# Tiles of their own for the first two inverse Haar sums, their places in the order, and earlier loads of the next coefficients

## Chip, cores and metric

One core of a Trainium2 chip. The metric is the device time of one execution in microseconds; the median of three runs is given. Engines are named as in the profile: PE (TensorE matmul), PEld (its weight loads), DVE (VectorE), ACT (ScalarE), POOL (GpSimd), SP (the queue that issues all DMAs here).

## What is computed

Four layers on a float32 image stack of 4 x 64 channels x 256 x 256. Layers 0, 2 and 3 are long 2D convolutions, separable per channel, with a residual; layer 1 is a Haar transform, a per-coefficient channel mixing with soft threshold, and the inverse transform:

```python
# layers 0, 2, 3: filters hx, hy come from small sine networks
k   = hx outer hy                          # one 256 x 256 filter per channel
y   = irfft2(rfft2(x) * rfft2(k))[:256, :256]
out = y + x * bias

# layer 1
f1 = haar2d(x)
for i in range(2):
    f4  = einsum('bchw,oc->bohw', f1 * v[i], conv_w[i])
    acc = acc + sign(f4) * relu(abs(f4) - tau[i])
out = haar2d(acc, inverse=True) + x
```

## The kernel before

**Rounds and groups.** Images are worked on in 64 rounds of 2 channels by 2 images (a tile `[128, 8, 256]`, 1 MB). Rounds 0 to 31 are group 0 (two images), 32 to 63 group 1. The channel mixing needs all channels of a group, so the coefficients go through DRAM: `coef[group]` before it, `mixed[group]` after it.

**Three phases**, each a list of small pieces that emit instructions:

- `phase_a`, the forward part, ten pieces a round (`A_PIECES`). In round t: convolution along rows of round t (`rows`, PE `a1ps`, evicted by ACT to `ay`), the Haar product of round t-3 (`product`, PE `a3ps`, evicted on DVE at L477 to `f`), convolution along columns of round t-1 (`columns`, PE `a2ps`, residual on DVE at L464 to `x1`), and, on POOL, the sums and differences of the Haar transform along the free dimension of round t-2 (`forward_free`, L344 and L346, 16 instructions, tiles `h128` to `h2`, result `fw`). The tail pieces are `a_last` (round 64, with the products of rounds 61 and 62, no rows any more) and `a_end` (forward sums and product of round 63, stores of 62 and 63).
- `phase_b(group)`, the mixing: load `ft` from `coef` and `v`/`tau`, matmul with the mixing matrix (L607), multiply, sign, magnitude, subtract, threshold (DVE and ACT), add on POOL, store to `mixed` (L675). It starts with a `join` of two steps on DVE (L579 to L586). Its pools are `b` and `bps` for group 0, `b2` and `bps2` for group 1.
- `phase_c`, the inverse part, 18 pieces a round (`C_PIECES`): load `g` from `mixed` (L755), scale it on ACT from round 2 on (`scales`, L362), the sums of the inverse Haar transform along the free dimension (`inverse_free`, 16 instructions in 8 levels, result `ci`), Haar product (PE `c0ps`, evicted by ACT to `z`), rows and columns of layer 2 (`c1r`, evicted to `ch`; `c1c`, residual to `cy`), the same for layer 3 (`c2r`, `c2c`), store. For rounds 0 and 1 the inverse sums run on DVE (L387, scaling inside), for later ones on POOL (L385).

**Order.** Each engine executes its instructions in the order in which they were emitted, and waits at the head of its queue. `beside(main, side, lead, tail)` emits a list of pieces and spreads a second list evenly among them. Most evictions are put off to the next piece (`later`, `flush`). The chain of calls at the end of the kernel is: forward pieces beside the filter networks; forward pieces beside the mixing of group 0; the last two rounds of forward pieces (62 and 63), with the first inverse rounds' loads and sums (`c_before`) among them; `a_last`; then the mixing of group 1 beside the inverse rounds.

**Buffers.** A tag of a pool is a ring of `bufs` tiles; a new tile waits until the last user of the one that it replaces has finished. What matters here:

- `in` (3): `x_t` of the forward rounds, then `g_t`, 1 MB each.
- `h2` to `h128` (1 each): the levels of `forward_free` *and* of `inverse_free`.
- PSUM: `acps`, a ring of 4 banks; `wide` or `wide2`, 2 banks more while they are open, taken in every third request; `bps`/`bps2` for the mixing.
- `v` (3), `m` (3), `x` (2) of pool `b`: the mixing's own, idle once it has ended.

`c_before` is `start` (load g_0 and g_1, the first Toeplitz filters, set up the sums of rounds 0 and 1) followed by eight lots of four inverse sums. `start` is emitted after piece (63, 3), the lots after pieces (63, 4) to (63, 7) and beside `a_last`. g_2 and g_3 are loaded in pieces 0 and 4 of inverse round 0.

Of the kernel before, what the change touches and what calls it, by code (L numbers as in the profile page):

```python
# [41 lines left out]
F32 = mybir.dt.float32  # L42
# [5 lines left out]
P = 128  # L48
B, C, N = 4, 64, 256

ROW = 64
BLOCKS = N // ROW
HALF = N // 2
# [13 lines left out]
NB = B // GROUPS  # L67
CI = 4 // NB
M = CI * NB
# [8 lines left out]
A_PIECES = 2 * BLOCKS + 2  # L78
C_PIECES = 4 * BLOCKS + 2
AHEAD = 3  # L80
SHRINK = (1, 2, 3, 5, 6, 10, 11, 12, 14, 15)
W = 2 * N
# [16 lines left out]
def conv_haar_kernel(  # L99
    ctx: ExitStack, tc: tile.TileContext, x, zT, w1, wbd, cols, wo, decay, wo_first, decay_first, bias, forward, inverse, wrow, pack, v, v_rows, out  # L100
):
    nc = tc.nc
# [15 lines left out]
    def pool(name, bufs, stack=ctx, **kw):  # L118
        return stack.enter_context(tc.tile_pool(name=name, bufs=bufs, reuse_waits="tile", **kw))

    ac = pool("ac", 2)
    acps = pool("acps", 4, space=PSUM)

    def big(tag, name, bufs):
        return ac.tile([P, 2 * M, N], F32, tag=tag, name=name, bufs=bufs)
# [24 lines left out]
    def load_toeplitz(l, t):  # L150

        both = ac.tile([P, SPAN - ROW], F32, tag="toep", name=f"toep{l}_{t}", bufs=4)
        for r in range(2):
            start = filt[l].offset + (t % ROUNDS * 2 + r) * REPEATS * SPAN
            src = bass.AP(filt[l].tensor, start, [[SPAN - 4, 16], [SPAN - 1, 4], [1, SPAN - ROW]])
            nc.sync.dma_start(both[r * ROW : (r + 1) * ROW], src)
        return both
# [122 lines left out]
    rest = []  # L282
# [68 lines left out]
    def diffs(src, half):  # L351

        if half < BLOCKS:
            return src.rearrange("p n (k q) -> p n k q", k=BLOCKS)[:, :, half : 2 * half, 0]
        m = half // BLOCKS
        return src.rearrange("p n (k q) -> p (n k) q", k=BLOCKS)[:, :, m : 2 * m]

    def scales(src):

        half = 2  # L360
        while half < N:
            nc.scalar.mul(diffs(src, half), diffs(src, half), math.sqrt(half))  # L362
            yield
            half *= 2

    def inverse_free(src, dst, name, engine):


        blocks = src.rearrange("p n (k q) -> p n k q", k=BLOCKS)

        cur, half = blocks[:, :, 0:1, 0], 1
        while half < N:
            o = dst
            if half < HALF:
                o = ac.tile([P, 2 * M, 2 * half], F32, tag=f"h{2 * half}", name=f"{name}{2 * half}", bufs=1)
            d = diffs(src, half)
            if half < BLOCKS:
                s, pair = cur, o.rearrange("p n (t q) -> p n t q", q=2)
            else:
                s = cur.rearrange("p n (k t) -> p (n k) t", k=BLOCKS)  # L380
                pair = o.rearrange("p n (k t q) -> p (n k) t q", k=BLOCKS, q=2)
            for q, op in ((0, ALU.add), (1, ALU.subtract)):
                to = pair[:, :, :, q]
                if engine is nc.gpsimd:
                    engine.tensor_tensor(to, s, d, op)  # L385
                else:
                    engine.scalar_tensor_tensor(to, d, math.sqrt(half) * (1 - 2 * q), s, ALU.mult, ALU.add)  # L387
                yield
            cur = o
            half *= 2  # L390
# [13 lines left out]
    def run(ops, count):  # L404
        for _ in range(count):
            next(ops, None)

    def all_rows(grp_tile, r, images, joined):

        parts = images.rearrange("(m q) (h n) k -> q m h (n k)", q=2, h=2)  # L410
        n = NB * W
        pairs = []
        for q in range(2):
            for h in (slice(0, 2),) if joined else (slice(0, 1), slice(1, 2)):
                at = grp_tile.offset + ((h.start * 2 + q) * ROUNDS + r) * n
                rows = [[PAIR, P // 2], [2 * ROUNDS * n, h.stop - h.start], [1, n]]
                pairs.append((bass.AP(grp_tile.tensor, at, rows), parts[q][:, h]))
        return pairs
# [321 lines left out]
    def phase_c():  # L740
# [3 lines left out]
        alone = total - ROUNDS  # L744
        stores = []
        st = [dict() for _ in range(total)]

        def load(t, k=slice(0, 4)):
            if t >= total:
                return  # L750
            if k.start == 0:
                st[t]["g"] = big("in", f"g_{t}", 3)
                st[t]["scales"] = scales(st[t]["g"])
            for rows, g in all_rows(mixed[t // ROUNDS], t % ROUNDS, st[t]["g"], False)[k]:
                nc.sync.dma_start(g, rows)  # L755
# [49 lines left out]
        def filters(t, l):  # L805
            if t < total:
                st[t]["toep", l] = load_toeplitz(l, t)

        def sums(t):
            if t < total:  # L810
                s = st[t]
                if t >= alone:
                    for h in range(2):
                        to, of = (s[k].rearrange("p (s n) k -> p s (n k)", s=2)[:, h] for k in ("g", "shrunk"))
                        nc.gpsimd.tensor_tensor(to, to, of, ALU.add)
                s["ci"] = big("t1", f"ci_{t}", 2)
                s["ops"] = inverse_free(s["g"], s["ci"], f"i{t}_", nc.vector if t < 2 else nc.gpsimd)

        def step(t, count):
            if t < total:  # L820
                run(st[t]["ops"], count)
# [62 lines left out]
        def piece(t, j):  # L884
            flush()
            if j == 0:
                if t == 0:
                    load(2)
                sums(t + 2)
            if t == 0 or t >= alone - AHEAD:  # L890
                if j == (BLOCKS if t == 0 else 1):
                    load(t + 3)
            elif j in (1, 3, 5, 7):
                load(t + 3, slice(j // 2, j // 2 + 1))
            if stores and j == C2 + BLOCKS + 3:
                stores.pop(0)()
            if j == 2:
                filters(t + 1, 1)
            if j == C2 + BLOCKS + 1 and t > 1:
                store(t - 2)  # L900
            if j == R2 + BLOCKS:
                filters(t, 2)
            first = t == alone - AHEAD
            if t >= alone - AHEAD:
                if j == 0 and first:
                    load_raw(alone)
                    load_rows()
                if j == 2 and first:
                    scale_rows()
                if j == BLOCKS + 1:  # L910
                    load_raw(t + AHEAD + 1)
                shrink(t + AHEAD, j - 2 * first)
            if R1 <= j < R1 + BLOCKS:
                if t < total:
                    rows(t, 1, j - R1)
            elif C2 <= j < C2 + BLOCKS:
                if 1 < t:
                    columns(t - 2, 2, j - C2)
            elif R2 <= j < R2 + BLOCKS:
                if 0 < t <= total:  # L920
                    rows(t - 1, 2, j - R2)
            elif j >= C1:
                if t < total:
                    columns(t, 1, j - C1)
            else:
                product(t + 1, int(j > BLOCKS))
            if t == 0:
                scaled(3, 2 * (2 * BLOCKS <= j < C1))
                scaled(2, int(j > 0))
            else:  # L930
                scaled(t + 3, {11: 3, 12: 2, 15: 1, 16: 1}.get(j, 0))
            if j > 0:
                step(t + 2, 1)
# [5 lines left out]
            sums(0)  # L939
            sums(1)  # L940

        before = [start] + [lambda t=t: step(t, 4) for t in range(2) for _ in range(4)]
        haar_first = [lambda h=h: (flush(), product(0, h)) for h in range(2)]

        pieces = [lambda t=t, j=j: piece(t, j) for t in range(total + 2) for j in range(C_PIECES)]
# [3 lines left out]
    def beside(main, side, lead, tail, weights=(1,)):  # L949


        weights = [weights[k % len(weights)] for k in range(len(main))]
        all_of = sum(weights[lead : len(main) - tail])
        done = 0
        for k, p in enumerate(main):
            p()
            want = len(side) * sum(weights[lead : k + 1]) // max(1, all_of)
            for q in side[done:want]:
                q()
            done = max(done, want)  # L960
# [4 lines left out]
    cut_a, cut_c = (ROUNDS + 2) * A_PIECES + BLOCKS + 4, (ROUNDS - AHEAD) * C_PIECES  # L965
# [4 lines left out]
    bp = pool("b", 2, during)  # L970
# [1 line left out]

    beside(a[cut_a : -2 * A_PIECES], phase_b(0), 2, 0)

    a, head = a[-2 * A_PIECES :], A_PIECES + BLOCKS
    beside(a[:head], c_before[:1], A_PIECES - 1, 0)
    beside(a[head:], c_before[1:5], 0, 2)
    beside(a_last, c_before[5:], 0, 5)
    during.close()
    bp = pool("b2", 2, during)  # L980
    rings[:] = [acps, acps, pool("wide2", 2, space=PSUM)]
    bps = pool("bps2", 2, during, space=PSUM)

    mid = 3 * BLOCKS + 2
    main = c_first + a_end[:1] + c[:BLOCKS] + c[mid:C_PIECES] + a_end[1:] + c[BLOCKS:mid] + c[C_PIECES:cut_c]
    beside(main, phase_b(1), len(c_first) + len(a_end) + 2 * BLOCKS, 0)
    during.close()
    late["sb"] = pool("late", 1)
    late["ps"] = pool("late_ps", 1, space=PSUM)
# [124 lines left out]
```

## Time and profile before

| | |
|---|---|
| runs, median (lowest to highest) | 2587.52 us (2584.11 to 2591.82) |
| profiled execution | 2585.35 us, span 2583.6 us |
| PE busy | 2319.3 us, 90% |
| POOL busy | 2064.4 us, 80% |
| DVE busy | 1823.0 us, 71% |
| ACT busy | 1324.7 us, 51% |
| DMA | 685.23 MB, 265 GB/s mean |
| chain that ended last | PE 60%, DVE 14%, POOL 10%, DMA 6%, issue 5% |

The busy shares are averages over the whole span. The mixing of group 0 ends at about 1065 us and the first mixing matmul of group 1 starts at 1161.42 us; the change concerns the stretch between. A timeline row gives start, length, engine, line, operation, output and input, count, and in brackets the idle time before it and what ended that.

### The profile page before, as it was taken

The numbers are of one execution on the slowest core, as the hardware profiler recorded it, in microseconds if no ns is written. First come the engines' busy times: TensorE is split into PE (matmuls) and PEld (weight loads), VectorE is DVE, ScalarE is ACT, GpSimd is POOL, SyncE is SP. The second block draws the span as 40 slices with busy tenths as digits, with TensorE's granted clock in tenths as the row PEclk, the third lists the DMA queues.
The fourth block names the chain that finished last, engine by engine and source line by source line (L and its number), as shares of the span: only waits on it lengthen the run. The fifth ranks groups of instructions, "written<-read, shape, count | busy, mean of one in ns | idle before, by whom it ended". The sixth has DMA issues, their size and how long they took to land.

```text
span 2583.6 us, 118458 instructions
## 1 busy us (share of the span) xinstructions
PE 2319.3 (90%) x53292; PEld 1848.1 (72%) x53292; DVE 1823.0 (71%) x2049; ACT 1324.7 (51%) x2187; POOL 2064.4 (80%) x2428
## 2 busy tenths in 40 slices
PE   5999999678888888757999999999989999999999
PEld 4877877444444444546777778777789998999998
DVE  2555445799999999646677777766757777777763
ACT  1221212566666666325666666666655655655552
POOL 1898887899989999767676777766779999999991
PEclk8999999899999999978999999999999999999999
DMA  7676998699999999555988999988876666666653
GB/s 210 216 244 234 298 309 283 243 342 323 337 340 316 351 321 330 182 194 194 331 301 309 317 320 323 313 306 297 288 233 211 223 213 212 221 216 208 219 166 111
DMA packets 203676, 685.23 MB, mean 265 GB/s; under 512 B 29289, under 2 KB 30826, under 8 KB 190755
## 3 DMA queue, kind: packets, MB, share of 16 engines
q1 hardware_dynamic: 203171, 677.67, 77.1%
q8 instruction: 418, 6.85, 1.1%
q14 instruction: 87, 0.71, 0.1%
HBM read 427.93 MB, written 249.63 MB: 262 GB/s over the span
## 4 chain that ended last, share of the span: by engine, by line
PE 60%; DVE 14%; POOL 10%; DMA 6%; issue 5%; ACT 3%; SPq 2%; DVEq 0%; ACTq 0%; POOLq 0%
PE c2c L296 11%; PE c2r L296 10%; PE c1r L296 9%; PE c1c L296 9%; PE a1ps L296 6%; PE a2ps L296 6%; PE f L607 4%; PE c0ps L308 4%; POOL fw L344 3%; DVE m L651 3%; POOL f L346 3%; DVE x L626 3%; DVE a L646 2%; PE a3ps L308 2%; DVE x L464 2%
## 5 line engine op out<-in xcount | busy, mean ns | idle before, releaser
L385 POOL TENSOR_TENSOR i<-i,g 128x16 f32<-128x16 f32 x744 | 431.5, 601 | 27.7 <-ACT g L362 0.6
L296 PEld LDWEIGHTS a2ps<-toep,ay 64*64 64x64 f32 x8192 | 305.5, 137 | 163.9 <-DVE f L477 86.4
L296 PE MATMUL a2ps<-toep,ay 64*64 64x128 f32 (+3 forms) x8192 | 357.7, 306 | 47.9 <-DVE f L477 42.3
L607 PE MATMUL f<-ft,mix 64*64 64x512 f32 x2048 | 297.3, 617 | 111.6 <-DVE x L626 94.3
L296 PEld LDWEIGHTS a1ps<-toep,x 64*64 64x64 f32 x8192 | 288.4, 134 | 89.7 <-issue 45.4
L296 PE MATMUL a1ps<-toep,x 64*64 64x64 f32 (+3 forms) x8192 | 337.6, 300 | 16.6 <-DMA x<-in_x 11.4
L296 PEld LDWEIGHTS c2c<-toep,ch 64*64 64x64 f32 x8192 | 300.0, 135 | 58.9 <-issue 19.1
L296 PE MATMUL c1r<-toep,z 64*64 64x192 f32 (+3 forms) x8192 | 319.0, 300 | 22.6 <-issue 11.9
L296 PEld LDWEIGHTS c1c<-toep,ch 64*64 64x64 f32 x8192 | 296.2, 134 | 57.8 <-issue 18.5
L296 PEld LDWEIGHTS c1r<-toep,z 64*64 64x64 f32 x8192 | 292.4, 135 | 59.2 <-issue 28.0
L296 PE MATMUL c2c<-toep,ch 64*64 64x256 f32 (+3 forms) x8192 | 314.7, 299 | 8.4 <-ACT ch L848 6.8
L296 PE MATMUL c1c<-toep,ch 64*64 64x128 f32 (+3 forms) x8192 | 310.3, 298 | 9.0 <-ACT ch L848 5.5
L669 POOL TENSOR_TENSOR gt<-m,ft 128x512 f32<-128x512 f32 x128 | 163.5, 1277 | 193.7 <-DVE m L651 188.8
L385 POOL TENSOR_TENSOR ci<-i,g 128x1024 f32<-128x1024 f32 x124 | 313.9, 2552 | 4.5
L444 ACT COPY ay<-a1ps 128x512 f32<-128x512 f32 x256 | 137.4, 589 | 351.2 <-PE a1ps L296 350.6
L296 PEld LDWEIGHTS c2r<-toep,cy 64*64 64x64 f32 x8192 | 287.9, 134 | 32.9 <-issue 15.2
L632 ACT ACTIVATE m<-x 128x1024 f32<-128x1024 f32 x194 | 206.1, 1062 | 205.3 <-DVE x L626 98.5
L296 PE MATMUL c2r<-toep,cy 64*64 64x192 f32 (+3 forms) x8192 | 310.1, 297 | 1.3 <-issue 1.1
L848 ACT COPY ch<-c2r 128x512 f32<-128x512 f32 x256 | 137.3, 591 | 280.2 <-PE c2r L296 279.5
L477 DVE TENSOR_TENSOR f<-a3ps,wrow_sb 128x512 f32<-128x512 f32 x256 | 161.3, 683 | 130.2 <-PE a3ps L308 130.2
L626 DVE TENSOR_TENSOR x<-f,v 128x1024 f32<-128x1024 f32 x192 | 233.5, 1216 | 22.1 <-PE f L607 20.5
L344 POOL TENSOR_TENSOR fw<-x 128x1024 f32<-128x1024 f32 x64 | 122.2, 1910 | 150.4 <-DVE x L464 137.9
(83 smaller groups left out, 3976.8 us busy)
## 6 DMA issues: line engine op xcount, KB each, us to landing
toep<-filt SPq DMA_DIRECT2D x384, 224.0 KB, 5.3
ft<-coef SPq DMA_DIRECT2D x128, 512.0 KB, 7.6
v<-in_v SPq DMA_DIRECT2D x64, 1024.0 KB, 10.1
mixed<-gt SPq DMA_DIRECT2D x128, 512.0 KB, 7.2
g<-mixed SPq DMA_DIRECT2D x256, 256.0 KB, 5.1
x<-in_x SPq DMA_DIRECT2D x128, 256.0 KB, 4.4
coef<-f SPq DMA_DIRECT2D x128, 256.0 KB, 4.0
x<-in_x SPq DMA_DIRECT2D x32, 1024.0 KB, 8.0
```

The costliest lines, as they stand in the source:

```text
L296: nc.tensor.matmul(ps[r][half(c), j % 2, k * ROW :], data[half(r), c, k, bass.ts(j, ROW)], t(r, c)[:, : N - k * ROW], start=k == 0, stop=k ...
L308: nc.tensor.matmul(ps[r][half(c)].rearrange("p h k -> p (h k)"), matrix[half(r)], pairs(r, c).rearrange("p h k -> p (h k)"), start=True, s ...
L344: nc.gpsimd.tensor_tensor(diffs, even, odd, ALU.subtract)
L346: nc.gpsimd.tensor_tensor(sums, even, odd, ALU.add)
L385: engine.tensor_tensor(to, s, d, op)
L444: later(lambda y=y, ps=ps: nc.scalar.copy(y, ps))
L477: later(lambda f=f, ps=ps, w=w: nc.vector.tensor_tensor(f, ps, w, ALU.mult))
L607: nc.tensor.matmul(un[u]["f4"][half(q), b, :], mixers[0][half(r), bass.ts(i, C)], st[s]["f"][half(r), b], start=True, stop=True, tile_posi ...
L626: nc.vector.tensor_tensor(un[u]["x"], un[u]["f4"], both(u, "v"), ALU.mult)
L632: nc.scalar.activation(un[u]["m"], un[u]["x"], AF.Sign)
L669: nc.gpsimd.tensor_tensor(g[:, 0], m[:, 0], st[s]["f"][:, 0], ALU.add)
L848: later(lambda y=y, ps=ps: nc.scalar.copy(y, ps))
```

## The change

- `inverse_free` takes a function `level(n)` that gives the tile of each level. For rounds 0 and 1 the levels are cut out of tiles with the tags `m` (level 128) and `x` (levels 2 to 64) of pool `b`; for later rounds they are the `h` tiles as before.
- g_0 and g_1 are tiles with the tag `v` of pool `b`, no longer of the ring `in`.
- The sums are emitted one at a time (32 steps of one) instead of four at a time: those of round 0 beside forward round 63, those of round 1 beside `a_last[1:]`.
- `start` moves ahead of piece (62, 0). The loads of g_2 and g_3 leave inverse round 0: g_2 goes ahead of piece (63, 0), g_3 behind `a_last[0]`.
- Pool `b` is closed, and `b2`, `bps2` and `wide2` are opened, after `c_first` (the two Haar products of inverse round 0) and `a_end[0]` (forward sums of round 63, store of 62), no longer ahead of them. The mixing of group 1 starts at the same piece as before.

```diff
-    def inverse_free(src, dst, name, engine):
+    def inverse_free(src, dst, name, engine, level):
...
-                o = ac.tile([P, 2 * M, 2 * half], F32, tag=f"h{2 * half}", name=f"{name}{2 * half}", bufs=1)
+                o = level(2 * half)
...
-            if k.start == 0:
+            if t < 2:
+                g = bp.tile([P, 2, 2, W], F32, tag="v", name=f"g_{t}", bufs=3)
+                st[t]["g"] = g.rearrange("p i k w -> p (i k w)").rearrange("p (n k) -> p n k", k=N)
+            elif k.start == 0:
                 st[t]["g"] = big("in", f"g_{t}", 3)
...
+        def levels(t):
+
+            if t >= 2:
+                return lambda n: ac.tile([P, 2 * M, n], F32, tag=f"h{n}", name=f"i{t}_{n}", bufs=1)
+            images = dict(n=2 * M)
+            most, rest = (bp.tile([P, NB, W], F32, tag=tag, name=f"i{t}_{tag}", bufs=n) for tag, n in (("m", 3), ("x", 2)))
+            most, rest = (k.rearrange("p b w -> p (b w)") for k in (most, rest))
+            cut = lambda k, at, n: k[:, at : at + 2 * M * n].rearrange("p (n k) -> p n k", **images)
+            return lambda n: cut(most, 0, n) if n == HALF else cut(rest, 2 * M * (n - 2), n)
...
             if j == 0:
-                if t == 0:
-                    load(2)
                 sums(t + 2)
-            if t == 0 or t >= alone - AHEAD:
-                if j == (BLOCKS if t == 0 else 1):
+            if t >= alone - AHEAD:
+                if j == 1:
                     load(t + 3)
+            elif t == 0:
+                pass
...
-        before = [start] + [lambda t=t: step(t, 4) for t in range(2) for _ in range(4)]
+        before = [start] + [lambda t=t: step(t, 1) for t in range(2) for _ in range(16)]
+        before += [lambda t=t: load(t) for t in (2, 3)]
...
-    a, head = a[-2 * A_PIECES :], A_PIECES + BLOCKS
-    beside(a[:head], c_before[:1], A_PIECES - 1, 0)
-    beside(a[head:], c_before[1:5], 0, 2)
-    beside(a_last, c_before[5:], 0, 5)
+    a = a[-2 * A_PIECES :]
+    c_start, c_sums, c_loads = c_before[0], c_before[1:-2], c_before[-2:]
+    half_way = len(c_sums) // 2
+    beside([c_start] + a[:A_PIECES], [], 0, 0)
+    beside([c_loads[0]] + a[A_PIECES:], c_sums[:half_way], 1, 0)
+    mid = 3 * BLOCKS + 2
+    beside(a_last[:1] + c_loads[1:] + a_last[1:] + c_first + a_end[:1], c_sums[half_way:], 2, 3)
     during.close()
     bp = pool("b2", 2, during)
...
-    mid = 3 * BLOCKS + 2
-    main = c_first + a_end[:1] + c[:BLOCKS] + c[mid:C_PIECES] + a_end[1:] + c[BLOCKS:mid] + c[C_PIECES:cut_c]
-    beside(main, phase_b(1), len(c_first) + len(a_end) + 2 * BLOCKS, 0)
+    main = c[:BLOCKS] + c[mid:C_PIECES] + a_end[1:] + c[BLOCKS:mid] + c[C_PIECES:cut_c]
+    beside(main, phase_b(1), len(a_end) - 1 + 2 * BLOCKS, 0)
```

More of the change, by code (lines that the diff above doesn't have):

```diff
@@ L816, in sums @@
                 s["ci"] = big("t1", f"ci_{t}", 2)
-                s["ops"] = inverse_free(s["g"], s["ci"], f"i{t}_", nc.vector if t < 2 else nc.gpsimd)
+                s["ops"] = inverse_free(s["g"], s["ci"], f"i{t}_", nc.vector if t < 2 else nc.gpsimd, levels(t))
         def step(t, count):
```

## The prediction

> **What bounds the kernel now.** I went from the page's forty slices (PE has one dip in its middle, slices 17 to 21) to the table by stretches around that dip, then to the waits inside it, then to the timeline of each engine. Columns of the first table: stretch, its length, busy us (and instructions) of PE, PEld, DVE, ACT and POOL, granted clock, DMA share, GB/s.
>
> ```profile
> 1060.00:1080.00 20.00, 19.67 (x472) 16.01 (x464) 8.62 (x13) 4.29 (x8) 19.29 (x23) 1.00 0.73 264
> 1080.00:1120.00 40.00, 21.99 (x306) 15.78 (x306) 24.32 (x52) 0.96 (x2) 15.29 (x30) 0.79 0.26 92
> 1120.00:1160.00 40.00, 24.19 (x413) 19.17 (x413) 12.19 (x16) 11.19 (x27) 28.69 (x48) 0.74 0.62 223
> ...
> 1300.00:1340.00 40.00, 36.80 (x859) 29.63 (x855) 28.02 (x27) 25.36 (x46) 26.79 (x36) 1.00 0.82 287
> ```
>
> From 1080 to 1160 PE is busy 46.2 of 80 us; a later stretch has it at 92%. At that share the hole would be 0.92 x 80 - 46.2 = 27 us shorter: **the ceiling** for the change, 1.1% of the span. No engine is full in the hole, so it is a chain. The waits from 1040 to 1185 (total us, times, longest):
>
> ```profile
> PE a2ps L296 <- DVE f L477: 16.9, 3, 10.2
> DVE i L387 <- POOL fw L346: 20.4, 2, 10.3
> PE c1r L296 <- ACT z L836: 10.6, 1, 10.6
> ACT g L362 <- DMA mix<-in_pack: 8.9, 1, 8.9
> ACT g L362 <- DMA toep<-filt: 8.3, 1, 8.3
> PE c1c L296 <- ACT ch L848: 5.2, 1, 5.2
> ```
>
> Four stalls of PE, in pairs. VectorE's inverse sums `i` twice wait 10 us for POOL's forward sums, because both take the `h` tiles, of which there is one each. The eviction `f` of a3ps stands behind them in VectorE's queue, and PE behind that:
>
> ```profile
> 1073.11 1.41 DVE L464 SCALAR_TENSOR_TENSOR x<-x,bias_sb,a2ps 128x512 f32<-128x512 f32 x2 [0.78 <-PE a2ps L296]
> 1084.83 0.26 DVE L387 SCALAR_TENSOR_TENSOR i<-g 128x8 f32<-128x8 f32 x2 [10.31 <-POOL fw L346]
> 1085.12 0.27 DVE L387 SCALAR_TENSOR_TENSOR i<-g,i 128x16 f32<-128x16 f32 x2
> 1085.31 1.28 DVE L477 TENSOR_TENSOR f<-a3ps,wrow_sb 128x512 f32<-128x512 f32 x2
> ```
>
> The other two are ACT scaling `g_2` and `g_3` before their loads (issued 1120.95 and 1142.93) have landed, with the copies of `ch` and `z` behind. The names "toep" and "mix" are only the DMA events nearest in time.
>
> **What the Trainium skill says.** "SBUF — State Buffer", section "Who interferes with whom": a VectorE instruction with two SBUF inputs contends with a GpSimd instruction that reads SBUF; one holds the shared ports for its whole length and the other is blocked. The trace agrees. The threshold at L651 is the same instruction in both groups; with one input in PSUM it is steady, with both in SBUF it is not (busy us, mean ns):
>
> ```profile
> L651 DVE SCALAR_TENSOR_TENSOR m<-a,m 128x1024 f32<-128x1024 f32 x128 | 156.2, 1220 | 5.5
> L651 DVE SCALAR_TENSOR_TENSOR m<-x,m 128x1024 f32<-128x1024 f32 x66 | 104.6, 1585 | 5.3 <-DVE x L646 0.5
> ```
>
> At 1239 the two engines are seen taking turns, first POOL's row, then VectorE's:
>
> ```profile
> 1238.14 6.61 POOL L385 TENSOR_TENSOR ci<-i,g 128x1024 f32<-128x1024 f32 x2
> ```
> ```profile
> 1239.32 3.20 DVE L651 SCALAR_TENSOR_TENSOR m<-x,m 128x1024 f32<-128x1024 f32 x1
> ```
>
> POOL's two sums (2.35 us each alone) take 6.61, and VectorE's one (1.22) takes 3.20, since it sits between them. The inverse sums at L387 have both inputs in SBUF; `f` (L477) and `x` (L464) have one in PSUM and stay at 0.68 and 0.74 us. "TensorE: Matmul & The Clock Gate", section "What's actually happening": after an idle window of about 3.4 us the PE clock is halved. The trace has 0.55 in 1084 to 1088, after 6.4 us idle, and `c1c` takes 7.2 us for its 128 matmuls at 1130 where a2ps took 4.6 at 1068.
>
> **The change part by part.** Times are of the profiled execution (2585.35 us, span 2583.6; the runs' median, 2587.52, lies 2.2 above).
>
> 1. *g_0 and g_1 into `v` buffers, issued before round 62.* Their buffers are free; what they need is the last `mixed` store, issued at 1064.92. DMA is quiet again at 1069 to 1071, so I let them issue at 1071: four at 0.6 us, 3.1 to landing, g_0 there at about 1076, g_1 at 1078.5. Behind these 8 DMAs and 2 toep loads on SP stand the coef stores of rounds 59 on (1069.73 before, now about 1078); the `f` buffer of round 59 is wanted again only at round 61's eviction, after 1094. Cost nothing; without that slack, 8 us.
>
> 2. *Inverse(0), one operation at a time beside round 63.* No `h` wait any more, so VectorE starts at 1076 instead of 1084.8. But POOL does forward(61) from 1074.8 to 1084.8, and eight small inverse sums stand ahead of the first `f`. Taking turns, each waits for one POOL sum: 1.85 + 1.86 + 1.04 + 1.0 + 0.6 + 0.6 + 0.4 + 0.4 = 7.8 us, and 8 x 0.14 of their own: done at 1083.7. `f` runs at 1083.8, against 1085.3: **1.5 us** gained where the wait was 10. Columns(62), its residual and the start of forward(62) (1096.05 before) go with it: about 1094.5.
>
> 3. *Inverse(1) beside round 64.* `f` of product(61) no longer waits for forward(62): at 1096 instead of 1106.6. Columns(63) follow 11 us earlier, overlapping forward(62). That ends at 1094.5 + 10 + about 1.2 for the sums between = 1105.7, so product(62) and forward(63) start 9 to 11 us earlier (forward(63) at about 1107.5, before 1118.5) and forward(63) ends at about 1120, before 1128.5.
>
> 4. *The last three inverse sums now stand ahead of the second `f` of product(62)* and meet forward(63)'s first POOL sums: 1107.5 + 1.85 + 0.66 + 1.87 + 1.22 + 1.05 + 1.22 = 1115.4, `f` 1116.6. c0ps' second half has only the four banks of `acps` now, since `wide2` opens later, so it waits for that `f`; PE is cold again. c1r ends at about 1125, as before (1125.0). **Steps 1 to 4 are worth about nothing at c1r**, bounds -2 to +15.
>
> 5. *g_2 and g_3 loaded earlier.* Their `in` buffers are those of x_61 and x_62, free at 1074.5 and 1095, so both land 20 to 40 us ahead of their scaling. The 5.2 us wait of c1c goes, and with it the half clock (7.2 to 4.6: 2.6 us): c1c, product(63) (forward(63) is done) and `f`(63) come **7.8 us** earlier, less up to 1 for the cold start: 7. What is late next is the store of coef(63): 4.0 us to land, then `ft`, the join, and the first mixing matmul (1161.4). The 10.6 us wait for `z` also goes, but PE then waits for that join instead, so I count nothing.
>
> 6. *g_3's 1 MB out of the queue between coef(63) and the mixing.* DMA is at 99 to 105% from 1144 to 1168 at some 365 GB/s: 2.7 us of it goes, and 3.3 us of SP's issue. I take **2.7**.
>
> 7. *Pool b closed two steps later.* The second mixing's tiles wait for inverse(1)'s last sum (1115), its loads come at 1135. Nothing. The same pieces follow in the same order, so a shift at the first mixing matmul stays to the end.
>
> Sum: 0 + 7 + 2.7 = about 10 us, 2585.35 - 10 = 2575; for the median, 2577.
>
> **Unknown cost.** No row shows small VectorE sums against a run of POOL sums. If they slip through without turns, steps 2 to 4 give back the two 10 us waits less 5 of remaining chain: 15 more, -25. If POOL holds the ports for its whole run, step 3's gain ends and `f`(62) comes after forward(63): +8, against -9.7. I take turns one for one, as at 1239, and keep both ends.
>
> **Rivals.** (A, 0.55) As summed: 2568 to 2581. (B, 0.20) Little port conflict: 2560 to 2567, near the ceiling; for it, the small sums last 0.14 us; against it, the 3.20 us row. (C, 0.13) The gain is swallowed: POOL holds the ports, or the join's loads set the mixing's start whatever is ahead; 2580 to 2590. For it, DMA at full share there; against, the 1 MB less. (D, 0.12) Slower: g_0 lands late. VectorE stands at the head of inverse(0), with `f`(60) and the residuals behind it and all of POOL's forward sums behind those; each us after about 1078 costs one, and beyond 1078 + 10 + 8 = 1096 the kernel loses over 0.3%. That needs 20 us to landing; the longest of the g loads took 10.0. At 1098: 2597.
>
> **How the numbers follow.** 0.3% (7.8 us, about what a measurement of this kernel can tell from no change) ends close to A's centre, so A gives 0.45 to faster and 0.10 to the same, B all to faster, C 0.02 to faster, 0.09 same and 0.02 slower, D 0.12 slower: 0.67, 0.19, 0.14. Point: 2577. Range: B's end at 2560 to C's at 2590, leaving part of D out.
>
> **What would show it.** Right: `i` no longer waits on POOL fw; forward(61) and `i` interleave, small `i` rows stretched; columns(63) near 1096; no ACT wait for g at 1121 and 1143; first mixing matmul near 1151. Wrong: `f`(60) already at 1079 (B); first `i` waiting for DMA g past 1085 (D); a first mixing matmul still past 1158 (C).

## The result and the profile after

The changed kernel takes 2565.2 us (median of 5 runs, 2557.88 to 2567.54) against 2584.11 of before (median of 5 as well, 2579.76 to 2591.82); the ratio is 0.9925, with a 95% interval of 0.9903 to 0.9946. Run a second time, on another occasion, it gave 0.9943 (0.9921 to 0.9964). It is faster, by 0.6 to 0.75%, which is 15 to 19 us; 10 were forecast.

The table by stretches of the kernel after, with the columns and the stretches of before:

```profile
1060.00:1080.00 20.00, 17.00 (x362) 13.14 (x358) 13.77 (x24) 3.26 (x7) 18.33 (x32) 0.95 0.80 285
1080.00:1120.00 40.00, 30.09 (x526) 21.47 (x522) 27.87 (x40) 6.71 (x15) 26.30 (x45) 0.85 0.36 128
1120.00:1160.00 40.00, 28.22 (x459) 19.32 (x453) 21.12 (x28) 19.35 (x38) 22.42 (x24) 0.83 0.70 241
```

PE is busy 58.3 of the 80 us from 1080 to 1160, where it was 46.2: the hole is shallower, not gone. Its waits, from the same view and window as before:

```profile
PE f L607 <- DVE ft L586: 8.1, 2, 7.2
...
PE a2ps L296 <- DVE f L477: 3.8, 2, 3.0
...
PE c1r L296 <- DVE f L477: 2.8, 1, 2.8
...
DVE i_x L387 <- DMA g<-mixed: 2.3, 1, 2.3
...
PE c2r L296 <- DMA toep<-filt: 2.0, 1, 2.0
...
PE c1r L296 <- ACT z L849: 1.9, 2, 1.7
...
ACT g L362 <- DMA g<-mixed: 0.5, 1, 0.5
```

The four old stalls of PE are small or gone: 16.9 has become 3.8, 10.6 has become 1.9, the 5.2 of c1c is gone, and ACT no longer waits for g_2 and g_3. New is the first line: PE waits for the join, which had been hidden behind the wait for `z`. Two smaller ones are new as well: c1r waits 2.8 us for `f`(62), and a3ps waits 3.6 us for POOL's forward sums.

**A measure that repeats.** The span fell by 27.5 us (2583.6 to 2556.1), more than the median. Part of that lies where the program is unchanged, so I measure the **stretch** between two marks, POOL's first sum of forward(61) and its first add of the second mixing. Before, then after:

```profile
1074.80 1.89 POOL L344 TENSOR_TENSOR fw<-x 128x1024 f32<-128x1024 f32 x1
...
1173.38 1.27 POOL L669 TENSOR_TENSOR gt<-m,ft 128x512 f32<-128x512 f32 x1 [12.30 <-DVE m L651]
```
```profile
1069.40 1.89 POOL L344 TENSOR_TENSOR fw<-x 128x1024 f32<-128x1024 f32 x1
...
1154.24 1.29 POOL L669 TENSOR_TENSOR gt<-m,ft 128x512 f32<-128x512 f32 x1 [17.03 <-DVE m L651]
```

The stretch is 98.6 us before and 84.8 after: 13.8 us less. Of the other 13.7 us of the span's difference, 5.4 lie ahead of the first mark and 8.0 between the first and the last add of the second mixing (703.2 and 695.3 us). The repeats, below, differ by as much from one execution to the next without any change, so neither is put down to the change.

### The profile page after: what moved, and what is told of

It is laid out like the page before. It is cut to its first block, busy times and chain, and to the rows that moved or that the text cites. A ratio compares the mean times of both kernels' runs of the same rounds, so it can differ in the third digit from the quotient of the medians.

```text
span 2556.1 us, 118462 instructions
## 1 busy us (share of the span) xinstructions
PE 2314.9 (91%) x53292; PEld 1788.5 (70%) x53292; DVE 1835.7 (72%) x2049; ACT 1324.5 (52%) x2187; POOL 2075.5 (81%) x2428
## 3 DMA queue, kind: packets, MB, share of 16 engines
q1 hardware_dynamic: 203171, 677.67, 77.3%
## 4 chain that ended last, share of the span: by engine, by line
PE 45%; DVE 5%; DMA 2%; issue 2%; ACT 2%; POOL 1%; SPq 0%; DVEq 0%; ACTq 0%; POOLq 0%
PE c2c L296 10%; PE c2r L296 10%; PE c1r L296 9%; PE c1c L296 8%; PE f L607 4%; PE c0ps L308 4%; DVE m L651 1%; DVE cy L880 1%; DVE x L646 1%; DVE x L626 1%; DMA g<-mixed 1%; ACT ch L861 0%; DMA toep<-filt 0%; DMA ft<-coef 0%; DMA rows<-in_v_rows 0%
## 5 line engine op out<-in xcount | busy, mean ns | idle before, releaser
L385 POOL TENSOR_TENSOR i<-i,g 128x16 f32<-128x16 f32 x744 | 437.3, 608 | 27.2
L296 PE MATMUL a2ps<-toep,ay 64*64 64x128 f32 (+3 forms) x8192 | 354.7, 305 | 30.5 <-DVE f L477 28.7
L296 PE MATMUL a1ps<-toep,x 64*64 64x64 f32 (+3 forms) x8192 | 340.7, 302 | 15.6 <-DMA x<-in_x 12.2
L296 PEld LDWEIGHTS c2c<-toep,ch 64*64 64x64 f32 x8192 | 279.5, 134 | 72.5 <-issue 36.9
L296 PEld LDWEIGHTS c1c<-toep,ch 64*64 64x64 f32 x8192 | 275.9, 133 | 69.5 <-issue 38.3
L296 PE MATMUL c1r<-toep,z 64*64 64x64 f32 (+3 forms) x8192 | 309.8, 299 | 14.9 <-issue 9.9
L296 PEld LDWEIGHTS c1r<-toep,z 64*64 64x64 f32 x8192 | 275.2, 135 | 60.7 <-issue 25.8
L296 PE MATMUL c2c<-toep,ch 64*64 64x128 f32 (+3 forms) x8192 | 306.7, 298 | 3.1 <-ACT ch L861 1.8
L296 PE MATMUL c2r<-toep,cy 64*64 64x192 f32 (+3 forms) x8192 | 302.8, 297 | 3.0 <-DMA toep<-filt 2.0
L296 PE MATMUL c1c<-toep,ch 64*64 64x128 f32 (+3 forms) x8192 | 301.0, 297 | 2.8 <-issue 2.8
L296 PEld LDWEIGHTS c2r<-toep,cy 64*64 64x64 f32 x8192 | 271.0, 134 | 46.0 <-issue 17.8
L880 DVE SCALAR_TENSOR_TENSOR o<-cy,bias_sb,c2c 128x512 f32<-128x512 f32 x256 | 176.7, 742 | 90.6 <-PE c2c L296 88.7
## 6 DMA issues: line engine op xcount, KB each, us to landing
v<-in_v SPq DMA_DIRECT2D x64, 1024.0 KB, 10.3
```

Source lines behind the costliest of these rows:

```text
L296: nc.tensor.matmul(ps[r][half(c), j % 2, k * ROW :], data[half(r), c, k, bass.ts(j, ROW)], t(r, c)[:, : N - k * ROW], start=k == 0, stop=k ...
L880: nc.vector.scalar_tensor_tensor(to, of, bias_sb[:, at : at + 1], ps, ALU.mult, ALU.add)
```

## Experiments

But for the repeats, all are edits of the changed kernel. Each has the stretch of one profiled execution and the ratio of its runs to the kernel before on the same occasion.

| kernel | stretch, us | ratio (95% interval) |
|---|---|---|
| before; again | 98.6; 98.1 | 1; 1.000 (0.9985 to 1.0015) |
| after; again | 84.8; 85.4 | 0.9925 (0.9903 to 0.9946); 0.9943 (0.9921 to 0.9964) |
| late_g | 94.4 | 0.9977 (0.9963 to 0.9990) |
| late_g3 | 90.4 | 0.9954 (0.9936 to 0.9972) |
| fours_h | 88.3 | 0.9969 (0.9955 to 0.9983) |
| in_ring | 94.1 | 0.9971 (0.9955 to 0.9987) |
| psum | 76.8 | 0.9908 (0.9874 to 0.9943) |
| later | 77.3 | 0.9925 (0.9900 to 0.9950) |
| later_psum | 79.1 | 0.9913 (0.9884 to 0.9941) |
| psum_order | 73.2 | 0.9891 (0.9874 to 0.9909) |

The intervals of psum, later and later_psum overlap those of the changed kernel, so the ratios alone don't rank these; the stretch does, where it differs by clearly more than it does between two executions of one kernel.

**Both kernels again** (no edit).

> The changed kernel once more, for a second profile and more times. The stretch from POOL's first sum of forward(61) to POOL's first add of the second mixing should be 84.8 us again, 13.8 below before. If the change acts in that stretch alone, the median of many runs lies 13 to 16 us below before and the 8 us that the first profile shows inside the second mixing (first to last add 695.3 us, before 703.2) are not there again: 698 to 705 us. If the change also speeds up the second mixing, it shows 694 to 697 us again and a total 19 to 22 us below before.

> The kernel before once more, for a second profile. Stretch 98.6 us again; first to last add of the second mixing: 703 us if that length belongs to the kernel, anywhere from 695 to 705 us if it differs from one execution to the next.

The stretch repeats to 0.6 us, in two pairs. First to last add of the second mixing took 704.6 us in the second profile of after (695.3 in the first) and 700.0 in that of before (703.2): it differs more from one execution to the next than between the kernels. No effect outside the stretch shows; the first profile happened to be of the fastest of its five runs.

**late_g: g_2 and g_3 late again.**

```diff
+                if t == 0:
+                    load(2)
                 sums(t + 2)
-            if t >= alone - AHEAD:
-                if j == 1:
+            if t == 0 or t >= alone - AHEAD:
+                if j == (BLOCKS if t == 0 else 1):
                     load(t + 3)
-            elif t == 0:
-                pass
...
-        before += [lambda t=t: load(t) for t in (2, 3)]
+        before += [lambda: None] * 2
```

> The changed kernel with one part undone: g_2 and g_3 are loaded in pieces 0 and 4 of inverse round 0 again; own tiles, v buffers and places of the sums stay. The measure is the stretch from POOL's first sum of forward(61) to POOL's first add of the second mixing: 98.6 us before, 84.8 after. Theory (the gain is two parts: some 4 us at c1r from the sums' own tiles, the rest from the loads): ACT waits for g_2 and g_3 again with the copies of ch and z behind, the stretch is about 92 us and the total some 7 us above the changed kernel. Rival (the own tiles carry the gain, the loads were covered): stretch 84 to 86 us, total as the changed kernel.

Measured: 94.4 us, 9.6 above the changed kernel. The waits from 1090 to 1170 have the old ones back:

```profile
ACT g L362 <- DMA g<-mixed: 21.0, 2, 12.5
...
PE c1r L296 <- ACT z L849: 10.5, 2, 10.3
```

The theory's waits are back, and the rival's 84 to 86 us are far off; the theory's own "about 92" was 2.4 us too low. With the sums' own tiles in place the two loads are worth 9.6 us of the 13.8, and all that is left of the change without them 4.2 (98.6 - 94.4).

**fours_h: the sums back in the `h` tiles at the old places, loads early.** The places are those of before but for round 1, whose 16 sums come in lots of 5, 5 and 6 instead of 4, 4 and 8.

```diff
-            if t >= 2:
+            if t >= 0:
                 return lambda n: ac.tile(...)
...
-    beside([c_loads[0]] + a[A_PIECES:], c_sums[:half_way], 1, 0)
+    head = A_PIECES + BLOCKS
+    beside([c_loads[0]] + a[A_PIECES:head], [], 0, 0)
+    beside(a[head:], c_sums[:half_way], 0, 2)
...
-    beside(a_last[:1] + c_loads[1:] + a_last[1:] + c_first + a_end[:1], c_sums[half_way:], 2, 3)
+    beside(a_last[:3], c_sums[half_way:], 0, 0)
+    beside(c_loads[1:] + a_last[3:] + c_first + a_end[:1], [], 0, 0)
```

> The changed kernel with the sums of inverse rounds 0 and 1 back in the h tiles, in lots, at the places of the kernel before; v buffers and early loads of g_2 and g_3 stay. Theory: both 10 us waits of DVE for POOL's forward sums are back, c1r ends about 50 us after the mark as before, the loads still give their 8 to 10 us: stretch 89 to 90 us, total some 5 us above the changed kernel. Rival (the own tiles carry the gain): stretch 97 to 98 us, total as before.

Measured: 88.3 us, a touch better than the theory's 89 to 90. The old wait of the sums is there in full while the stretch is 10.3 us below before (waits, 1070 to 1150):

```profile
DVE i L387 <- POOL fw L346: 20.4, 2, 10.3
```

So 20 us of DVE's wait, which is the first thing that catches the eye in the profile of before, were worth 3.5 us of the stretch (88.3 - 84.8), and the early loads, with the `v` buffers, 10.3 alone. That these two make 13.8 is so by construction; the test is the other order, late_g, with 4.2 and 9.6. The two orders agree to 0.7 us, about what the stretch differs by between executions.

**late_g3: only g_3 late.**

```diff
             elif t == 0:
-                pass
+                if j == BLOCKS:
+                    load(3)
...
-        before += [lambda t=t: load(t) for t in (2, 3)]
+        before += [lambda: load(2), lambda: None]
```

> The changed kernel with g_3 alone loaded in piece 4 of inverse round 0 again; g_2 stays early. late_g, with both late, had a stretch of 94.4 us against 84.8 to 85.4. The prediction gave g_2 7 us (the wait of ch at c1r and the cold clock behind it) and g_3 2.7 us (its 1 MB and SP's issues in front of ft). Theory as predicted: stretch 87 to 89 us. Rival (g_3 costs more, since the copy of z stands behind its scaling and the row convolution behind that): 90 to 94 us.

Measured: 90.4 us, in the rival's band: at the end of the stretch g_3 is worth 5 to 5.6 us and g_2 the remaining 4.0 (94.4 - 90.4), where I had 2.7 and 7. Cut into its parts, the stretch shows where each acts (us):

| | before | late_g | late_g3 | after |
|---|---|---|---|---|
| mark to c1r's end | 50.2 | 47.3 | 47.4 | 45.9 |
| to the end of `f`(63) | 16.5 | 14.9 | 8.8 | 8.8 |
| to the first mixing matmul | 19.9 | 19.9 | 19.8 | 15.1 |
| to the first add of the mixing | 12.0 | 12.4 | 14.3 | 15.1 |

g_2 gives 6.1 us in the second row, g_3 4.8 in the third. The last row takes back 1.9 and 0.8 of them. The 1.5 us of the first row can't be put down to the loads, since no wait there names them; c1r's matmuls, behind their wait, had a granted clock of 0.60 and 0.63 in the two late runs (1110 to 1118 and 1113 to 1121), and of 0.73 and 0.72 in the two profiles of after (1109 to 1115 and 1111 to 1117).

The rival was right on the size and not on the way: PE's wait for `z` is back with 10.5 us, but the join ends later still, so that the first mixing matmul waits for the join and not for `z`. What g_3 does beside SP and DMA is seen at the join, whose eight operations on the first image stand ahead of the first mixing matmul. The first rows are DVE and then POOL of late_g3:

```profile
1145.11 1.48 DVE L585 TENSOR_TENSOR ft<-spare_f 64x256 f32<-64x256 f32 x1
1146.52 2.58 DVE L586 TENSOR_TENSOR ft<-spare_f 64x256 f32<-64x256 f32 x1
```
```profile
1143.74 2.57 POOL L385 TENSOR_TENSOR i<-i,g 128x512 f32<-128x512 f32 x2
1146.39 2.42 POOL L385 TENSOR_TENSOR ci<-i,g 128x1024 f32<-128x1024 f32 x1
```

And the same two operations of the join in the changed kernel:

```profile
1138.38 0.41 DVE L585 TENSOR_TENSOR ft<-spare_f 64x256 f32<-64x256 f32 x1
1138.72 0.41 DVE L586 TENSOR_TENSOR ft<-spare_f 64x256 f32<-64x256 f32 x1
```

With g_3 late, POOL's inverse sums of round 3 are late too and take turns with the end of the join. With g_3 early they are over by 1137.2, and meet its beginning only: there L581 still takes 2.56 us, where for the second image it takes 0.42. From the join's first operation to the first mixing matmul it is 9.4 us before, 9.3 in late_g3, 6.2 in the changed kernel; the join of the second image, with POOL idle, takes 2.9.

**in_ring: g_0 and g_1 in the ring `in`.**

```diff
-            if t < 2:
-                g = bp.tile([P, 2, 2, W], F32, tag="v", name=f"g_{t}", bufs=3)
-                st[t]["g"] = ...
-            elif k.start == 0:
+            if k.start == 0:
```

> The changed kernel with g_0 and g_1 back in the ring in; the levels' own tiles, the places of the sums and of the loads stay. g_1 then waits for x_62, g_2 for x_63 and g_3 for g_0, and the stores of coef stand behind them in SP's queue. Theory (the v buffers pay because the early loads need the slots of x_61 and x_62): g_2's load waits for the residual of round 63, some 28 us after the mark, store(60) behind it, and f(62) waits for that store; stretch 88 to 93 us. Rival (only the places of the loads matter): 84 to 86 us.

Measured: 94.1 us, 1.1 above the theory's band. The direction is the theory's, the place is one round earlier than I had it. SP's queue, then VectorE's `f`(61):

```profile
1069.79 22.09 SPq L755 DMA_DIRECT2D g<-mixed  x8
1091.92 1.23 SPq L158 DMA_DIRECT2D toep<-filt  x2
1093.19 1.32 SPq L481 DMA_DIRECT2D coef<-f  x2
```
```profile
1100.55 1.29 DVE L477 TENSOR_TENSOR f<-a3ps,wrow_sb 128x512 f32<-128x512 f32 x2 [9.75 <-DMA coef<-f]
```

g_1's load waits for x_62 and holds SP for 22 us; store(59) comes behind it, and `f`(61), which takes the buffer of `f`(59), runs 30.5 us after the mark instead of 18.8. g_0 itself also lands later, and VectorE waits 7.4 us for it instead of 2.3. Without the `v` buffers 9 us are lost: the early issue of the loads blocks the stores.

**psum: the levels in PSUM.**

```diff
-            most, rest = (bp.tile([P, NB, W], F32, tag=tag, name=f"i{t}_{tag}", bufs=n) for tag, n in (("m", 3), ("x", 2)))
-            most, rest = (k.rearrange("p b w -> p (b w)") for k in (most, rest))
+            held = {}
+            def whole(tag):
+                if tag not in held:
+                    held[tag] = bps.tile([P, NB, W], F32, tag=tag, name=f"i{t}_{tag}", bufs=1).rearrange("p b w -> p (b w)")
+                return held[tag]
...
-            return lambda n: cut(most, 0, n) if n == HALF else cut(rest, 2 * M * (n - 2), n)
+            return lambda n: cut(whole("f4"), 0, n) if n == HALF else cut(whole("a"), 2 * M * (n - 2), n)
```

> The changed kernel with the levels of inverse rounds 0 and 1 in PSUM (the mixing's two PSUM tiles, idle by then), so that 28 of 32 DVE sums have one input in SBUF only and the other in PSUM; order and loads stay. Theory (the DVE sums are stretched because they take turns with POOL's forward sums at the shared SBUF ports): the sums run near their length alone (0.14 to 0.7 us), the last two of inverse(1) still write ci from PSUM without waiting, 2.4 us instead of 5.6; f of product(60) some 2 us earlier, f(62) some 4 us earlier, stretch 80 to 82 us. Rival (the stretching comes from dependences between the sums, or is off the chain): lengths as in the changed kernel, stretch 84 to 86 us.

Measured: 76.8 us, 8.0 below the changed kernel, more than expected. Groups of the inverse sums (busy us, mean ns of one), first of the kernel before, in which POOL stood idle beside them, then of the changed kernel, then of psum:

```profile
L387 DVE SCALAR_TENSOR_TENSOR ci<-g,i 128x1024 f32<-128x1024 f32 x4 | 4.7, 1224 | 0.1
...
L387 DVE SCALAR_TENSOR_TENSOR i<-g,i 128x16 f32<-128x16 f32 x4 | 0.5, 175 | 0.1
L387 DVE SCALAR_TENSOR_TENSOR i<-g 128x8 f32<-128x8 f32 x4 | 0.5, 172 | 20.4 <-POOL fw L346 20.4
```
```profile
L387 DVE SCALAR_TENSOR_TENSOR ci<-g,i_m 128x1024 f32<-128x1024 f32 x4 | 8.0, 2038 | 0.1
L387 DVE SCALAR_TENSOR_TENSOR i_x<-g 128x8 f32<-128x8 f32 x4 | 2.8, 749 | 2.3 <-DMA g<-mixed 2.3
...
L387 DVE SCALAR_TENSOR_TENSOR i_x<-g,i_x 128x16 f32<-128x16 f32 x4 | 1.9, 502 | 0.0
```
```profile
L387 DVE SCALAR_TENSOR_TENSOR ci<-g,i_f 128x1024 f32<-128x1024 f32 x4 | 4.7, 1222 | 0.1
L387 DVE SCALAR_TENSOR_TENSOR i_a<-g 128x8 f32<-128x8 f32 x4 | 3.9, 965 | 3.2 <-DMA g<-mixed 3.1
...
L387 DVE SCALAR_TENSOR_TENSOR i_a<-g,i_a 128x16 f32<-128x16 f32 x4 | 0.7, 183 | 0.1
```

With one input in PSUM the sums run about as long as they did before, with POOL idle. The smallest, 128x8, has both inputs in `g`, thus in SBUF, in both kernels, and is stretched in both: a control inside the experiment. So the cause of the stretching is that both inputs lie in SBUF while POOL works, and not a dependence between the sums, which is the same in both kernels. Taking turns with POOL costs the changed kernel some 8 us.

**later: the sums behind the evictions.**

```diff
-    beside([c_loads[0]] + a[A_PIECES:], c_sums[:half_way], 1, 0)
+    beside([c_loads[0]] + a[A_PIECES:], [], 1, 0)
...
-    beside(a_last[:1] + c_loads[1:] + a_last[1:] + c_first + a_end[:1], c_sums[half_way:], 2, 3)
+    beside(a_last[:1] + c_loads[1:] + a_last[1:], c_sums[:half_way], 2, 2)
+    beside(c_first + a_end[:1], c_sums[half_way:], 0, 0)
```

> The changed kernel with the sums moved: none beside round 63; those of round 0 beside a_last, those of round 1 beside c_first and a_end[0], behind the evictions that they stood ahead of. Theory (the evictions f(60) and f(62) and the residual of round 62 stand behind the inverse sums in DVE's queue, and forward(62) and c1r start from them): the residual of round 62 is done some 7 us earlier, forward(62) starts with it, c1r ends 10 to 12 us earlier, stretch 72 to 77 us, total some 10 us below the changed kernel. Rival (POOL's three forward sums and the join's loads set the stretch whatever stands in DVE's queue): stretch 83 to 86 us, total as the changed kernel.

Measured: the stretch is 77.3 us, at the theory's edge; forward(62) starts 11.5 us after the mark (19.0 in the changed kernel), and c1r ends 9.0 us earlier. The total does not show it: 0.9925 (0.9900 to 0.9950) is the ratio of the changed kernel too, so the gain of this run rests on the stretch of one profile.

**later_psum: both.**

> The changed kernel with both: levels in PSUM and the sums moved behind the evictions as in the run later. In later the residual of round 63 stood behind inverse(0)'s sums, which took turns with forward(62). Theory: without the turns that residual is done before forward(62) ends (22 us after the mark), forward(63) starts at 22 to 24 instead of 29, c1r ends some 5 us earlier, stretch 70 to 73 us, total 26 to 30 us below before. Rival (the two gains are the same one, or the join's loads bind): stretch 76 to 78 us.

Measured: 79.1 us, 2 us worse than either alone, outside the bands of theory and rival; my theory missed what was next. PE's timeline has it:

```profile
1102.33 5.10 PE L296 MATMUL c1r<-toep,z 64*64 64x256 f32 x126
1111.04 5.33 PE L296 MATMUL c1c<-toep,ch 64*64 64x256 f32 x97 [3.60 <-DVE ci L387]
```

c1c waits for the last inverse sum, which ends at 1110.89 and on which it has no data to wait for. What they share, by the program, is PSUM: the levels lie in the two tiles of `bps`, and `wide2` and `bps2` are opened over them. In psum and in the kernel below, in which the sums end earlier, c1c follows c1r without a wait.

**psum_order: PSUM levels, evictions first, levels given back in time.** Edit to psum:

```diff
-    beside([c_loads[0]] + a[A_PIECES:], c_sums[:half_way], 1, 0)
+    beside([c_loads[0]] + a[A_PIECES:], c_sums[:12], 7, 0)
...
-    beside(a_last[:1] + c_loads[1:] + a_last[1:] + c_first + a_end[:1], c_sums[half_way:], 2, 3)
+    beside(a_last[:1] + c_loads[1:] + a_last[1:] + c_first + a_end[:1], c_sums[12:], 2, 3)
```

> The run psum with the sums of inverse round 0 moved: the first twelve beside the last pieces of round 63, behind both evictions of product(60), the last four (the two long levels) and all of round 1 beside a_last[1:]. In later_psum the sums of round 1 held the PSUM tiles until 38.2 us after the mark, and c1c, whose banks lie there, waited for them; here they end ahead of the Haar products as in psum. Theory (evictions first, no turns, PSUM given back in time): forward(62) starts 12 us after the mark instead of 15.7, c1r 2 to 4 us earlier than in psum, stretch 72 to 75 us. Rival (in psum the stretch is already set by what comes behind c1r): 76 to 78 us.

Measured: 73.2 us, and 2555.51 us in all, ratio 0.9891 (0.9874 to 0.9909): **better than both kernels**: its six runs (2552.05 to 2561.12) lie below all eleven of the changed kernel but one (2557.88). forward(62) starts 12.2 us after the mark, c1r 29.2 (32.7 in psum). Its stretch is 25.4 us below before, close to the 27 that the prediction estimated as the ceiling.

## Why the prediction was right, and where it was off

The direction and the range (2560 to 2590) hold, and so does the mechanism of the likeliest case, A: a gain cut down by turns with POOL. Its number holds only in part. 2565.2 lies outside A's 2568 to 2581 and inside the band of rival B, whose mechanism the traces refute; on the second occasion the ratio of 0.9943, applied to 2587.5, gives 2573, in A's band. The sum was 10 us; the stretch shows 13.8. By its steps, in us after the first mark:

| | before | after | gain | forecast |
|---|---|---|---|---|
| step 2, `f`(60) | 10.5 | 7.1 | 3.4 | 1.5 |
| step 2, forward(62) starts | 21.2 | 19.0 | 2.2 | 1.5 |
| step 3, forward(63) starts | 43.7 | 33.3 | 10.4 | 11 |
| step 4, c1r ends | 50.2 | 45.9 | 4.3 | 0 |
| step 5, `f`(63) ends | 66.7 | 54.7 | 12.0 | 7 |
| step 6, first mixing matmul | 86.6 | 69.8 | 16.8 | 9.7 |
| first add of the mixing | 98.6 | 84.8 | 13.8 | 10 |

- **Step 1** held: VectorE started 2.0 us after the mark, 1.2 forecast.
- **Step 2 was mis-sized**: the eight small sums took 5.2 us, not 7.7. Most do not take turns one for one:

```profile
1071.39 1.87 DVE L387 SCALAR_TENSOR_TENSOR i_x<-g 128x8 f32<-128x8 f32 x2 [2.27 <-DMA g<-mixed]
1073.29 3.33 DVE L387 SCALAR_TENSOR_TENSOR i_x<-g,i_x 128x16 f32<-128x16 f32 x6
```

  The first two end at 1073.26, just behind a POOL sum (1071.26 to 1073.15): one waits, the second slips through behind it. The next two pairs do the same (1.00 and 0.17 us, 0.92 and 0.19); the last two sums, 0.57 and 0.65 us, wait for one POOL sum each. So eight sums cross five POOL sums, and forward(61) took 10.0 us as before; the second profile has the same pattern. The long ones do take turns: forward(63)'s first three POOL sums, 1.89, 1.89 and 1.04 us alone, with the two `ci` sums between them (POOL, then VectorE):

```profile
1102.66 2.04 POOL L344 TENSOR_TENSOR fw<-x 128x1024 f32<-128x1024 f32 x1 [3.67 <-issue]
1104.66 2.87 POOL L346 TENSOR_TENSOR f<-x 128x1024 f32<-128x1024 f32 x1
1107.61 1.90 POOL L344 TENSOR_TENSOR fw<-f 128x512 f32<-128x512 f32 x1
```
```profile
1102.99 5.63 DVE L387 SCALAR_TENSOR_TENSOR ci<-g,i_m 128x1024 f32<-128x1024 f32 x2
1108.54 1.28 DVE L477 TENSOR_TENSOR f<-a3ps,wrow_sb 128x512 f32<-128x512 f32 x2
```

- **Step 3** held to 0.6 us. That it held although step 2 was off is no contradiction: forward(62) came only 0.7 us earlier than forecast.
- **Step 4** had the mechanism, `f`(62) behind the last sums, visible just above, but its size was 4.3 us off, inside its bounds of -2 to +15. `f`(62) came about 4.4 us earlier than before, where I had 2; and it is c1r, not the second half of c0ps, that waits for it (2.8 us).
- **Step 5** held: from c1r's end to `f`(63) 16.5 us became 8.8, a gain of 7.7 for the 7 forecast. By late_g and late_g3, g_2 is 6.1 of it. At the end of the stretch only 4.0 of these are left.
- **Step 6 was mis-sized**: it gave 4.8 us up to the first mixing matmul instead of 2.7, and late_g3 shows that all of it is g_3's. The missing term is POOL's inverse(3), which overlaps the join less: 3.2 us of it. The rest, 1.6, is what the queue gave, less than the 2.7. (The rate behind the 2.7 was misread: from 1144 to 1168 the trace of before has 343 GB/s on average, not 365.)
- **Step 7 failed in part**: it let a shift at the first mixing matmul stay to the end, but from there to the first add 12.0 us became 15.1. Two things lie there. c2r waits 2.0 us for its `toep` load, which SP issued behind the mixing's own loads, and the next mixing matmul stands behind c2r. And PE, which had been idle for 7.2 us, runs the first eight mixing matmuls at a granted clock of 0.50 (1139 to 1144; before, 1.00 from 1160 to 1164). The first six, before and then after:

```profile
1161.42 1.08 PE L607 MATMUL f<-ft,mix 64*64 64x512 f32 x6 [0.25 <-DVE ft L586]
```
```profile
1139.18 1.98 PE L607 MATMUL f<-ft,mix 64*64 64x512 f32 x6 [7.16 <-DVE ft L586]
```

  late_g3 has such a wait for `toep` (1.7 us) and fast matmuls, and takes 14.3 us; psum has the slow matmuls and hardly the wait (0.3 us), and takes 14.2. So each seems to count; they were not tried apart.
- **Luck in the sum**: the two loads were forecast at 7 + 2.7 = 9.7 us and late_g gives 9.6. But g_2 was a little less and g_3 nearly twice as much, and step 7, forecast at nothing, took back most of the difference. The tiles and places of the sums, forecast at about nothing, gave 3.5 to 4.2 us, which is what the sum of 10 lacks.
- **The rivals**: B (little conflict with POOL) is refuted by psum, and the turns were worth 8 us there, not the 15 of the prediction; C (the gain swallowed) is present only as the 3 us of step 7; D (g_0 late) did not happen, DVE waited 2.3 us for it.

## What to carry to other kernels

A wait of 20 us at the head of a queue was worth some 4 us, and two loads issued earlier 10: follow what stands behind each wait before valuing it. When VectorE work with two SBUF inputs is laid beside a run of GpSimd sums, try one input in PSUM, or a place behind the evictions that PE waits for; here the first alone gave 8 us more, and together with the right order 11.6. If scratch is put into PSUM, count when its banks are wanted again.

## What was not expected of the hardware

In these traces short VectorE sums (0.17 us alone) mostly passed in pairs behind one GpSimd sum: forward(61) took 10.0 us with eight of them as without. Where longer ones, up to 128x256, were among them, forward(62) took 10.6 us. Sums of 1.22 us alternated one for one, and two of them delayed GpSimd's next three sums by 2.0 us. Writing and reading the levels in PSUM cost VectorE next to nothing: 691 ns against 689 for 128x512, 1222 against 1224 for 128x1024, 183 against 175 for 128x16.
